# A rarely taken branch as rolled loops, and weight folds moved around it, in a two-layer attention and feed-forward kernel

## The chip, the cores and the metric

The kernel runs on one core of a Trainium2 chip. The metric is device microseconds of one execution, taken as the median of several runs. In the profile, PE is the matmul engine, PEld its weight loads, DVE the vector engine, ACT the scalar engine, POOL GpSimd, and SP the engine that issues most DMAs. A float32 matmul of the program appears as two matmul records (two passes) and two weight loads; a transpose on PE appears as one.

## The reference, cut to what matters

Eight sequences of 100 tokens, 512 wide, pass two layers. Each layer adds an attention over a context of 361 rows and then a feed-forward part.

```python
x = x + L0_xattn(layernorm(x), ctx, Wq, Wkv_expand, Wout)     # 16 heads, causal mask
x = x + L0_ffn(layernorm(x), Wg, W1, W2, W3)                  # 8 experts, best 2 of them
x = x + L1_xattn(layernorm(x), ctx, Wq, w_kc_q, w_kc_kv, W_qr, W_kr, Wo)
x = x + L1_ffn(layernorm(x), w_gate_up, w_down)               # 8-bit quantised
```

The first feed-forward part is a mixture of experts:

```python
topk_s, topk_i = top_k(x @ Wg.T, 2)
w = softmax(topk_s) spread over the 8 experts, 0 elsewhere
for e in range(8):
    y += w[..., e:e+1] * ((silu(x @ W1[e].T) * (x @ W2[e].T)) @ W3[e].T)
```

In the second attention the queries pass three matrices of a head one after the other, `Wq` (512 to 128), `w_kc_q` (128 to 384) and `W_qr` (384 to 64). Nothing stands between them, so the kernel multiplies the matrices first ("folds" them) and applies one matrix of 512 x 64 per head. The last feed-forward part uses weights that are rounded to integers row by row with a scale of their own.

## The kernel before

**Tokens and tiles.** The 800 tokens lie in seven tiles of 128 rows (the last has 32), `xs[0]` to `xs[6]`. Everything up to the experts is written in a fixed order for PE, DVE and ACT (`tc.manual_schedule`); POOL and SP are ordered by the framework's scheduler, which places a DMA where it expects its operands to be ready. Each engine then runs its own instructions strictly in the order of its program. SP's DMAs each also wait until the DMA eight before has completed.

**First attention.** Two matmuls with zeros (L433) come before the first data. Tile by tile, rows are normalised on DVE (`first_norm`), turned on PE and copied by ACT into `xnT` (`token_columns`, L253 and L254). `queries0(b, n)` (L257) makes the queries of `n` batches at once: its matmuls (L269) have `n` x 100 columns, and ACT scales and copies them (L273). Before, batches 0 and 1 are made one at a time, all others two at a time. Batch 0 needs token tile 0 alone, batch 1 tiles 0 and 1.

**Choices and slots.** `rank_choices` finds the two best experts of each token on DVE, and `give_slots` gives every choice one of 240 slots (`CAP`) of its expert; fourteen indirect DMAs of POOL (L680) write the rows into the DRAM array `x_slot`. The flag `spilt` (L806) says whether some expert has more than 240 choices. `values_load` (L879) brings it into registers of PE, DVE, ACT and POOL, and under `tc.If` (L886) a general path (L887 to L950) computes the choices without a slot: every expert over every token tile, unrolled in full, 56 times the body. With these inputs no choice is without a slot; no instruction of lines 887 to 950 but the branch itself is in the trace. Behind the branch SP reads the slot rows of experts 0 and 1 (`fetch`, L960), waiting for the last scatter.

**Folds.** Heads are folded in eight pairs, in three steps: `fold_head` for each head of a pair (L705, twelve passes of 64 columns for the pair) and a copy by ACT (L713), `fold_second` (L723, the two heads into the two column halves of the array; copy L727), and `fold_third` (four transposes, L733; copy L734) into `wqf`. `fold_load` brings a pair's matrices by SP: `wq_p` 512 KB, `kq_p` 2 x 192 KB, `qr_p` 2 x 96 KB; each has three buffers. Pair 0 is folded ahead of the branch. Of pair 1 the first step runs ahead of it (its second half is written behind it, at L1037, but the built program has all twelve passes ahead). Behind the branch come the rest of pair 1 and the whole of pair 2, then the transposes of expert 0's rows (L985), then the experts; pairs 3 to 7 are folded inside experts 0 to 4.

**Experts.** For each expert PE makes three chunks of gate and up products (`gate_and_up`, L1053), with a fold step after each, then turns the next expert's rows (L985) and multiplies by `w3` (L1117). ACT does Silu (L1064, L1072), DVE the product `hT` (L1065, L1073 to L1077). Beside it DVE quantises weights of the last feed-forward part: two rows of tiles of `w_gate_up` in each expert (`quantise_next`) and in experts 0 to 3 one tile of `w_down`, 704 KB (`quantise_down`, three long DVE instructions of 1.6, 0.95 and 0.9 us on tile `dn`, which has one buffer). DVE does that quantisation between the second and the third chunk's `hT`. SP turns each quantised tile by a DMA transpose (L150) and loads the next. SP's queue also carries the weights of the expert after the next (`load_expert`: w12 1408 KB, w3 three parts), its slot rows, the fold pairs, and `load_wo`, the output weights of the second attention, of which heads 5 to 7 use the buffers of the fold pairs.

**Later stages** (second attention, last feed-forward) follow at about 285 us.

Of the kernel before, what the change touches and what calls it, by code (L numbers as in the profile page):

```python
# [12 lines left out]
F32 = mybir.dt.float32  # L13
BF16 = mybir.dt.bfloat16
I32 = mybir.dt.int32
# [4 lines left out]
P = 128  # L20
# [30 lines left out]
def tile_kernel(  # L51
# [19 lines left out]
    def bank(dtype=F32):  # L71
        cols = 512 if dtype == F32 else 1024
        return psum.tile([P, cols], dtype, tag="bank", name="bank")
# [22 lines left out]
    SPARE = 2 * P  # L96
    x_slot = tc.dram_tile([1 + NE * CAP + 2 * NR, W], F32, name="x_slot")
    x_acc = tc.dram_tile([NR + SPARE, D], F32, name="x_acc")
    ctx_rot = tc.dram_tile([B, LP, LC, DC], F32, name="ctx_rot")
    scale_row = tc.dram_tile([OT + KC, P], F32, name="scale_row")  # L100
    xs = [keep.tile([P, D], F32, tag=f"x{t}", name=f"x{t}") for t in range(NT)]
# [155 lines left out]
    def queries0(b, n, parts=(0, 1)):  # L257
        per = 4 // n
        if parts[0] == 0:
            qT = atw.tile([P, KC, n * S], F32, tag=f"qT{n}", name=f"qT{b}")  # L260
            for i in range(n):
                queries_of[b + i] = qT[:, :, ts(i, S)]
                halves_of[b + i] = qT
        qT = halves_of[b]
        for o0 in [per * i for i in parts if per * i < KC]:
            pq = bank()
            for o in range(o0, o0 + per):
                for c in range(KC):
                    nc.tensor.matmul(  # L269
                        pq[:, ds((o - o0) * n * S, n * S)], wq_sb[:, c, ts(o, P)],  # L270
                        xnT[:, c, ds(b * S, n * S)], start=(c == 0), stop=(c == KC - 1),
                    )
            nc.scalar.activation(  # L273
                qT[:, ds(o0, per), :], pq[:, : KC * S].rearrange("p (c q) -> p c q", c=per),
                AF.Copy, scale=1.0 / math.sqrt(HD0),
            )
# [152 lines left out]
        attn0_values(b, vals.pop(b), pT)  # L429


    for _ in range(2):
        nc.tensor.matmul(bank()[:, :384], zeros[:, :P], zeros[:, :384], start=True, stop=True)  # L433
    first_norm(0, 1)
    take_columns(0)
# [1 line left out]
    first_norm(1, 2)  # L437
    keys(0, 2, KC)
    take_columns(1)
    queries0(0, 1)  # L440
    queries0(1, 1)
    first_norm(2, NT)

    begin(0)
# [257 lines left out]
    def fold_head(i, wq_p, kq_p, qr_p, j, pa=None):  # L702
        pa = bank() if pa is None else pa
        for c in range(CQ // P):
            nc.tensor.matmul(  # L705
                pa[:, ts(j, R1)], kq_p[:, j, c, :], qr_p[:, j, c, :],
                start=(c == 0), stop=(c == CQ // P - 1),
            )
        return pa

    def fold_copy(i, wq_p, kq_p, qr_p, pa):
        a_p = fw.tile([P, 2 * R1], F32, tag="a_p", name=f"a_p{i}", bufs=2)
        nc.scalar.copy(a_p, pa[:, : 2 * R1])  # L713
        return i, wq_p, a_p

    def fold_first(*loads):
        pa = fold_head(*loads, 0)
        return fold_copy(*loads, fold_head(*loads, 1, pa))

    def fold_second(i, wq_p, a_p):  # L720
        pb = bank()
        for j in range(2):
            nc.tensor.matmul(  # L723
                pb[ds(R1 * j, R1), :], a_p[:, ts(j, R1)], wq_p[:, j, :], start=True, stop=True
            )
        f_p = fw.tile([P, D], F32, tag="f_p", name=f"f_p{i}", bufs=2)
        nc.scalar.copy(f_p, pb)  # L727
        return i, f_p
# [61 lines left out]
    fold_third(*part)  # L790
    gate_scores(5, 7, xT)

    loads = loaded.pop(0)
    pa = fold_head(*loads, 0)
    rank_choices(5, 7)
    give_slots(5, 7)

# [6 lines left out]
    nc.vector.tensor_reduce(most, pn[:, :NE], AX.X, ALU.max)  # L804
    spilt = gp.tile([P, 1], I32, tag="spilt", name="spilt")
    nc.vector.tensor_scalar(spilt, most, float(CAP), None, ALU.is_gt)  # L806
    close_atw()
    close_at()

# [60 lines left out]
    def slot_tiles(e):  # L870
# [9 lines left out]
        spilt[0:1, 0:1], min_val=0, max_val=1,  # L880
        engines=[
            mybir.EngineType.PE, mybir.EngineType.DVE, mybir.EngineType.Activation,
            mybir.EngineType.Pool,
        ],
    )
    with tc.If(spills > 0, preferred_fallthrough_block=False):  # L886
        sp, close_sp = open_pool("spill", side="right")  # L887
        wts = sp.tile([P, NT, NE], F32, tag="wts", name="wts")
        for k in range(2):
            nc.vector.scalar_tensor_tensor(  # L890
                probs[k], slot1[k], 0.0, probs[k], ALU.is_equal, ALU.mult
            )
            nc.vector.tensor_tensor(
                hots[k], hots[k], probs[k].unsqueeze(2).to_broadcast([P, NT, NE]), ALU.mult
            )
        nc.vector.tensor_tensor(wts, hots[0], hots[1], ALU.add)
        for t in range(NT):
            nc.vector.memset(xs[t], 0.0)
        for e in range(NE):
            c3 = sp.tile([P, 3, D], F32, tag="sp3", name=f"sp3_{e}")  # L900
            for m, (m0, mr) in enumerate(HCH):
                nc.gpsimd.dma_start(c3[:mr, m, :], w3[e, ds(m0, mr), :])
            for t, r in enumerate(ROWS):
                pt = bank().rearrange("p (c q) -> p c q", c=KC)
                for c in range(KC):
                    nc.tensor.transpose(
                        pt[:, c, :r], x_all[:r, t, ts(c, P)], ident[:r, :r]
                    )
                xT = sp.tile([P, KC, P], F32, tag="spx", name=f"spx{e}_{t}")
                nc.scalar.copy(xT[:, :, :r], pt[:, :, :r])  # L910
                hT = sp.tile([P, 3, P], F32, tag="sph", name=f"sph{e}_{t}")
                for m, (m0, mr) in enumerate(HCH):
                    pw = bank()
                    ups = [(0, UP[m], mr)] if m < 2 else [(0, UP64, 64), (64, HE, 32)]
                    for j, cols in enumerate(([(0, m0, mr)], ups)):
                        a = sp.tile([P, KC, P], F32, tag=f"sp{j}", name=f"sp{j}_{e}_{t}_{m}")
                        for to, at_col, n in cols:
                            nc.gpsimd.dma_start(
                                a[:, :, ds(to, n)],
                                w12[e, :, ds(at_col, n)].rearrange("(c p) h -> p c h", p=P),  # L920
                            )
                        for c in range(KC):
                            nc.tensor.matmul(
                                pw[:mr, ds(j * P, r)], a[:, c, :mr], xT[:, c, :r],
                                start=(c == 0), stop=(c == KC - 1),
                            )
                    s = sp.tile([P, P], F32, tag="sps", name="sps")
                    nc.scalar.activation(s[:mr, :r], pw[:mr, :r], AF.Silu)
                    nc.vector.tensor_tensor(
                        hT[:mr, m, :r], s[:mr, :r], pw[:mr, ds(P, r)], ALU.mult  # L930
                    )
                py = bank()
                for m, (m0, mr) in enumerate(HCH):
                    nc.tensor.matmul(
                        py[:r, :D], hT[:mr, m, :r], c3[:mr, m, :], start=(m == 0), stop=(m == 2)
                    )
                nc.vector.scalar_tensor_tensor(
                    xs[t][:r], py[:r, :D], wts[:r, t, e : e + 1], xs[t][:r], ALU.mult, ALU.add
                )

        for xg in (*first_tiles[0], *first_tiles[1]):
            nc.gpsimd.memset(xg[0:1, 0:1], 0.0)
        row = sp.tile([P, NT], I32, tag="row", name="row")
        nc.gpsimd.iota(row, pattern=[[P, NT]], base=0, channel_multiplier=1)
        for t, r in enumerate(ROWS):
            nc.gpsimd.indirect_dma_start(
                out=x_acc, out_offset=bass.IndirectOffsetOnAxis(ap=row[:r, t : t + 1], axis=0),
                in_=xs[t][:r], in_offset=None, compute_op=ALU.add,
            )
        close_sp()  # L950

    close_gp()
# [81 lines left out]
    )  # L1034
    in_order.__enter__()

    part = fold_copy(*loads, fold_head(*loads, 1, pa))  # L1037
    following = fold_first(*loaded.pop(0))
    part = fold_second(*part)
    following = fold_second(*following)  # L1040
# [5 lines left out]
    for e in range(NE):  # L1046
# [35 lines left out]
        part = None  # L1082
        gate_and_up(0)
        if loaded:
            part = fold_first(*loaded.pop(0))
            if pairs_left:
                loaded.append(fold_load(pairs_left.pop(0)))
        quantise_next()
        gate_and_up(1)
        if part:  # L1090
            part = fold_second(*part)
        if e < KC:
            turn_down(*quantise_down(*down_in))
            if e + 1 < KC:
                down_in = load_down(e + 1)
        gate_and_up(2)
        quantise_next()
        if e + 2 < NE:
            experts[e + 2] = load_expert(e + 2)
        else:  # L1100
            load_wo(*((0, 1, 2) if e + 2 == NE else (3, 4)))
        if part:
            fold_third(*part)
        if e == KC + 1:
            load_wo(5, 6, 7)
        if e + 1 < NE:
            turned = columns_of(e + 1, slots[e + 1])
            gates_next = choices(e + 1, slots[e + 1])

        py = [bank() for _ in range(HC)]  # L1110
        down = [(m, i) for m in range(len(HCH)) for i in range(HC)]
# [617 lines left out]
```

## Time and profile before

| | |
|---|---|
| median of 3 runs | 683.59 us (680.39 to 683.71) |
| profiled execution | 684.2 us, of which the span is 682.5 us |
| mean granted PE clock | 0.981 |
| PE / DVE / ACT / POOL busy | 95% / 62% / 36% / 27% of the span |
| spilt flag ready on DVE (L806) | 129.16 us |
| last scatter issued (L680), first slot rows fetched (L960) | 132.96 us, 135.79 us |
| PE's first instruction behind the branch | 134.65 us |
| first product of expert 0 (L1053) | 144.27 us |
| experts 0, 1, 2 in the chain (start to next start) | 18.4, 18.2, 18.2 us |
| experts 3, 4 | 21.2, 18.4 us |
| experts 5, 6 (no fold) | 15.2 us each |

Times of instructions are counted from the span's start, and all come from the one profiled execution. A row of the timeline gives start, duration, engine, line, operation, tiles and count, and in brackets the idle time before it with what ended it. A row of the question by source line gives least, median and greatest duration in ns. A row of the windows gives, for a stretch, the busy time and number of instructions of PE, PEld, DVE, ACT and POOL, then the granted PE clock, the DMA share (1.0 when all 16 DMA engines are busy) and GB/s. DMA work that an instruction starts is not inside that instruction's duration. PE's busy time counts modelled ends, so neighbouring rows overlap a little; the chain of waits counts each stretch once.

### The profile page before, as it was taken

How to read it: one execution, taken by the hardware profiler on the slowest of the kernel's cores; microseconds unless marked ns; L12 is line 12 of the kernel's file. 1: busy time of each engine (PE TensorE's matmuls, PEld its weight loads, DVE VectorE, ACT ScalarE, POOL GpSimd, SP SyncE). 2: the span in 40 equal slices, each digit the busy share in tenths (PEclk: the TensorE clock that was granted, in tenths of full speed). 3: DMA queues.
4: the chain of work that ended last, by engine and by line, in shares of the span. 5: the costliest groups of instructions: out<-in, count | busy, mean ns of one | idle time of the engine just before them, and what ended most of it. 6: DMA issues, size and time to landing. Idle time of an engine off the chain costs nothing.

```text
span 682.5 us, 10210 instructions
## 1 busy us (share of the span) xinstructions
PE 647.0 (95%) x3637; PEld 417.3 (61%) x3637; DVE 420.7 (62%) x1059; ACT 245.2 (36%) x557; POOL 184.1 (27%) x197
## 2 busy tenths in 40 slices
PE   8999997499998999999999999999999999999995
PEld 6767755367765677568866666666666644444442
DVE  4875698326665453254168877776676356566687
ACT  3654444141221211231155555455555322221140
POOL 2222231601110022138424243324333102221021
PEclk9999999589999999999999999999999999999998
DMA  8700293699999999664200211110000120111211
GB/s 303 237 17 18 99 331 108 244 301 190 271 288 321 322 254 275 131 193 122 63 1 17 57 44 42 31 35 12 1 11 1 46 83 8 30 29 30 49 37 61
DMA packets 80312, 80.41 MB, mean 118 GB/s; under 512 B 41283, under 2 KB 54135, under 8 KB 80127
## 3 DMA queue, kind: packets, MB, share of 16 engines
q1 hardware_dynamic: 76543, 70.97, 35.8%
q0 software_dynamic: 3712, 8.72, 6.6%
q8 instruction: 30, 0.49, 0.3%
q14 instruction: 27, 0.22, 0.1%
HBM read 56.36 MB, written 16.50 MB: 107 GB/s over the span
## 4 chain that ended last, share of the span: by engine, by line
PE 65%; DVE 7%; DMA 3%; POOL 2%; issue 2%; ACT 1%; SPq 0%; POOLq 0%; ACTq 0%; DVEq 0%
PE bank L357 12%; PE bank L1053 10%; PE bank L1333 10%; PE bank L1312 7%; PE bank L1267 6%; PE bank L1117 5%; PE bank L1327 4%; PE bank L1457 3%; POOL e L1321 2%; PE bank L1300 2%; DVE nm L1314 1%; PE bank L705 1%; PE bank L723 1%; DMA dn<-in_wdn 1%; PE bank L985 1%
## 5 line engine op out<-in xcount | busy, mean ns | idle before, releaser
L1321 POOL TENSOR_SCALAR e<-e,rs 128x361 f32<-128x361 f32 (+1 forms) x56 | 67.3, 1203 | 134.9 <-DVE rs L1320 134.2
L357 PE MATMUL bank<-wvo,ctxT 128*128 128x512 f32 x192 | 83.9, 593 | 0.0
L1312 PE MATMUL bank<-kvT,qe 128*128 128x361 f32 (+1 forms) x208 | 82.0, 477 | 0.0
L1053 PE MATMUL bank<-xgT,w 128*128 128x240 f32 (+1 forms) x384 | 76.5, 371 | 1.6 <-ACT xgT L989 0.9
L1053 PEld LDWEIGHTS bank<-xgT,w 128*128 128x128 f32 (+1 forms) x384 | 63.8, 181 | 16.7 <-issue 9.0
L1333 PE MATMUL bank<-pT,kvr 121*128 121x400 f32 x192 | 70.4, 502 | 1.8 <-DVE pT L80 1.8
L1318 ACT ACTIVATE e<-bank,nm 128x361 f32<-128x361 f32 (+1 forms) x104 | 58.7, 564 | 29.8 <-DVE nm L1314 21.0
L1327 PEld LDWEIGHTS bank<-ident,e 128*121 128x121 f32 (+1 forms) x312 | 47.3, 183 | 33.7 <-POOL e L1321 7.8
L1314 DVE TENSOR_REDUCE nm<-bank 128x1 f32<-128x361 f32 (+1 forms) x104 | 54.9, 528 | 20.3 <-PE bank L1312 19.2
L357 PEld LDWEIGHTS bank<-wvo,ctxT 128*128 128x128 f32 x192 | 36.2, 190 | 43.1 <-issue 42.6
L1128 POOL DMA_INDIRECT x_acc<-y,place x16 | 24.4, 1525 | 128.5 <-ACT y L1127 125.0
L1327 PE MATMUL bank<-ident,e 128*121 128x128 f32 (+1 forms) x312 | 52.8, 279 | 2.1 <-POOL e L1321 2.1
L1474 POOL TENSOR_TENSOR hid<-g,u 128x512 f32<-128x512 f32 (+1 forms) x17 | 20.5, 1214 | 111.1 <-ACT g L1465 74.8
L1333 PEld LDWEIGHTS bank<-pT,kvr 121*128 121x128 f32 x192 | 33.9, 190 | 21.3 <-issue 1.9
L1117 PE MATMUL bank<-w,hT 128*128 128x512 f32 (+3 forms) x96 | 43.3, 596 | 2.2 <-DVE hT L1077 2.2
L1267 PE MATMUL bank<-xT,wqf 128*128 128x256 f32 (+1 forms) x192 | 43.8, 389 | 0.7 <-ACT xT L1252 0.7
L322 POOL TENSOR_TENSOR s<-s,rs 100x800 f32<-100x800 f32 x16 | 24.4, 1523 | 71.2 <-DVE rs L321 30.5
L1267 PEld LDWEIGHTS bank<-xT,wqf 128*128 128x128 f32 x192 | 36.2, 190 | 7.4 <-ACT xT L1252 0.9
L1312 PEld LDWEIGHTS bank<-kvT,qe 128*128 128x128 f32 (+1 forms) x208 | 32.5, 186 | 9.4
L82 ACT COPY pT<-bank 121x384 f32<-121x384 f32 (+1 forms) x51 | 23.7, 465 | 31.9 <-PE bank L1327 31.3
L80 DVE COPY ctxT<-bank 128x400 f32<-128x400 f32 (+2 forms) x23 | 13.2, 574 | 34.1 <-PE bank L1267 24.8
L1117 PEld LDWEIGHTS bank<-w,hT 128*128 128x128 f32 (+3 forms) x96 | 16.8, 183 | 22.9 <-issue 16.4
(251 smaller groups left out, 1020.2 us busy)
## 6 DMA issues: line engine op xcount, KB each, us to landing
w<-in_w SPq DMA_DIRECT2D x8, 1408.0 KB
gu<-in_wgu SPq DMA_DIRECT2D x22, 256.0 KB
w<-in_w SPq DMA_DIRECT2D x16, 256.0 KB
wq_p<-in_wq SPq DMA_DIRECT2D x8, 512.0 KB
wo<-in_wo SPq DMA_DIRECT2D x8, 512.0 KB
x_slot<-zeros SPq DMA_DIRECT2D x1, 3840.0 KB
kq_p<-in_wkcq SPq DMA_DIRECT2D x16, 192.0 KB
dn<-in_wdn SPq DMA_DIRECT2D x4, 704.0 KB
```

The costliest lines, as they stand in the source:

```text
L322: nc.gpsimd.tensor_tensor(part, part, rs.unsqueeze(2).to_broadcast([S, 8, S]), ALU.mult)
L357: nc.tensor.matmul(po[:, :D], lhs[:, c, ds(t * P, r)], rhs[:, c, :], start=(c == 0), stop=(c == chunks - 1),)
L1053: nc.tensor.matmul(po, w12_e[:, c, cols], xgT[:, c, :], start=(c == c0), stop=(c == c1 - 1))
L1117: nc.tensor.matmul(py[i][:n], hT[:mr, m, ds(s0, n)], w3_e[:mr, m, :], start=(m == 0), stop=(m == 2))
L1128: d = nc.gpsimd.indirect_dma_start(out=x_acc, out_offset=bass.IndirectOffsetOnAxis(ap=place[:, 0:1], axis=0), in_=y, in_offset=None, compu ...
L1267: nc.tensor.matmul(pq[:, i, :], wqf[:, c, ts(p0 + i, P)], xT[:, c, :], start=(c == 0), stop=(c == KC - 1),)
L1312: nc.tensor.matmul(ps[:r, :L], qe[:, ds(k0, r)], kvT, start=True, stop=True)
L1314: d = nc.vector.tensor_reduce(nm[:r], ps[:r, :L], AX.X, ALU.max, negate=True)
L1318: nc.scalar.activation(e[:r], ps[:r, :L], AF.Exp, bias=nm[:r], accum_out=sm[:r])
L1321: (nc.vector if odd else nc.gpsimd).tensor_scalar_mul(e[:r], e[:r], rs[:r])
L1327: nc.tensor.transpose(pt[:LP, c, :r], e[:r, ds(c * (LP - 1), LP)], ident[:r, :r])
L1333: nc.tensor.matmul(pc[:, :VC], kvr[:, c, :], pT[:, c, ts(j, VC)], start=(c == 0), stop=(c == LC - 1))
```

## The change

1. One more matmul with zeros at the start (three for two).
2. Queries of batches 0 and 1 are made together, as those of the later batches.
3. Pair 1 is folded whole ahead of the branch: first step before `rank_choices(5, 7)`, second and third after the flag is computed. Behind the branch stand pairs 2 and 3; pairs 4 to 7 are folded in experts 0 to 3, and expert 4 has none.
4. Inside the experts the first step has new functions. `fold_beside` swaps the operands: `qr_p` (64 columns) is now the weight and `kq_p` (128 columns) streams, and the two heads of a pair go into the two column halves of the array. The result lies turned, so `fold_turn` turns it back: one transpose and one more copy by ACT per pair. Each later step of a pair moves one place down: the second step after the third chunk, the third after the next expert's transposes.
5. The general path is written as two rolled loops over experts and token tiles, with gathers by indirect DMA, and adds into `x_acc` directly. SP takes part in the branch, so it too loads the flag. The body is now the path that falls through.
6. ACT runs a Silu on one column behind the branch, which the built program places ahead of it together with its table load.

```diff
-    for _ in range(2):
+    for _ in range(3):
         nc.tensor.matmul(bank()[:, :384], zeros[:, :P], zeros[:, :384], start=True, stop=True)
...
-    queries0(0, 1)
-    queries0(1, 1)
+    queries0(0, 2)
...
+    def fold_beside(i, wq_p, kq_p, qr_p):
+        pa = bank()
+        for c in range(CQ // P):
+            for j in range(2):
+                nc.tensor.matmul(
+                    pa[ds(R1 * j, R1), :P], qr_p[:, j, c, :], kq_p[:, j, c, :],
+                    start=(c == 0), stop=(c == CQ // P - 1),
+                )
+        t_p = fw.tile([P, P], F32, tag="t_p", name=f"t_p{i}", bufs=1)
+        nc.scalar.copy(t_p, pa[:, :P])
+        return i, wq_p, t_p
+
+    def fold_turn(i, wq_p, t_p):
+        pa = bank()
+        nc.tensor.transpose(pa[:, :P], t_p, ident)
+        a_p = fw.tile([P, P], F32, tag="a_p", name=f"a_p{i}", bufs=2)
+        nc.scalar.copy(a_p, pa[:, :P])
+        return i, wq_p, a_p
...
-    loads = loaded.pop(0)
-    pa = fold_head(*loads, 0)
+    part = fold_first(*loaded.pop(0))
     rank_choices(5, 7)
     give_slots(5, 7)
...
+    part = fold_second(*part)
+    fold_third(*part)
     close_atw()
...
-            mybir.EngineType.Pool,
+            mybir.EngineType.Pool, mybir.EngineType.SP,
...
-    with tc.If(spills > 0, preferred_fallthrough_block=False):
+    with tc.If(spills > 0, preferred_fallthrough_block=True):
...
-            for t, r in enumerate(ROWS):
+        with tc.For_i(0, NE, 1, hint_engines=()):
...
+            with tc.For_i(0, NT, 1, hint_engines=()):
+                x_t = sp.tile([P, D], F32, tag="spx", name="spx")
+                gathered(x_t, x_all_rows, at_x)
...
-    part = fold_copy(*loads, fold_head(*loads, 1, pa))
+    nc.scalar.activation(most, ln_eps, AF.Silu)
+    part = fold_first(*loaded.pop(0))
     following = fold_first(*loaded.pop(0))
...
         gate_and_up(0)
         if loaded:
-            part = fold_first(*loaded.pop(0))
+            part = fold_beside(*loaded.pop(0))
...
         gate_and_up(1)
         if part:
-            part = fold_second(*part)
+            part = fold_turn(*part)
...
         gate_and_up(2)
+        if part:
+            part = fold_second(*part)
         quantise_next()
...
-        if part:
-            fold_third(*part)
...
             turned = columns_of(e + 1, slots[e + 1])
             gates_next = choices(e + 1, slots[e + 1])
+        if part:
+            fold_third(*part)
```

The order of SP's DMAs is not written by hand. In the built program it shifts inside the experts: before, SP's queue in expert 2 reads turned `dn` tile 2, load of `dn` tile 3, turned and loaded `w_gate_up` tiles, w12 of expert 4; after, it reads load of a `wo` part, w12 of expert 4, turned `dn` tile 2, load of `dn` tile 3. Likewise in expert 1: before, turned `dn` tile 1, load of `dn` tile 2, and then w12 of expert 3; after, `wq_p` of pair 7, w12 of expert 3, turned `dn` tile 1, load of `dn` tile 2. In expert 0, w12 of expert 2 stands ahead of `dn` tile 1 in both; after, `wq_p` of pair 6 stands ahead of it too.

## The prediction

> **What bounds the kernel now.** I read the page's busy shares first (PE 95% of 682.5 us), then the 40 slices, where the granted clock falls to 5 and 8 tenths in slices 8 and 9 (119 to 153 us) and the DMA share is full from slice 10 to 15. So two stretches matter: the branch, and the experts behind it. The rows on the branch, from the questions by source line and by time:
>
> ```profile
> L886 ACTq COMPARE_BRANCH  x2: 38/44/49, 130.0 to 130.1; - x2
> L886 PEldq COMPARE_BRANCH  x2: 89/1917/3745, 130.4 to 130.7; - x2
> ...
> 134.65 2.64 PEld L705 LDWEIGHTS bank<-qr_p,kq_p 128*128 128x128 f32 x12 [8.12 <-issue]
> 137.40 3.74 PE L723 MATMUL bank<-wq_p,a_p 128*64 128x512 f32 x8
> 142.37 0.98 PE L985 MATMUL bank<-ident,xg 128*128 128x128 f32 x8
> ```
>
> PE's second branch instruction, a jump over the body of the general path, holds PE for 3.745 us; ScalarE's takes 49 ns. PE restarts at 134.65, cold (granted clock 0.50 from 121 to 141), and the folds then run without a gap into the first expert's transposes.
>
> Behind it the chain of waits, cut to its pieces, shows the one place where an expert does not wait for PE:
>
> ```profile
> 199.09 3.45 PE bank L1053 x16
> ...
> 204.44 7.48 DMA dn<-in_wdn
> ...
> 211.94 1.63 DVE amax L145
> ```
>
> ```profile
> 156.00:158.00 2.00, 2.00 (x16) 1.70 (x15) 1.89 (x5) 1.44 (x3) 0.00 (x0) 1.00 0.35 52
> 188.00:196.00 8.00, 8.00 (x42) 4.81 (x41) 5.47 (x10) 2.40 (x5) 0.00 (x0) 1.00 1.11 313
> 196.00:204.00 8.00, 8.00 (x38) 5.77 (x37) 5.13 (x16) 1.21 (x3) 3.04 (x2) 1.00 1.15 270
> ```
>
> The last row of `w_down` lands at 211.92. VectorE, in written order, cannot multiply expert 3's third hidden chunk before it has quantised that row, and PE stands 1.89 us at L1117. Expert 3 took 21.2 us (199.1 to 220.3), experts 1 and 2 took 18.2. The last two columns of the windows are DMA share and GB/s: in 188 to 204 the queue is full, in 156 to 158 it has a hole. So from 135.8 on one DMA queue, SP's, runs beside PE, and expert 3 ends when the queue has got through its list.
>
> **The change part by part.** *Start.* The third warm-up product costs two passes of 0.73 us (L433, 4 in 2.93) and lies in PE's 1.32 us gap before L253: 0.14 us too long. The queries of batches 0 and 1 go from 64 passes in 7.29 us (L269, 10.25 to 17.54) to 32 passes, which for batches 2 and 3 took 5.68. But they now need tile 1's columns, and ScalarE's copy of them ends at 11.03; before, batch 0 ran ahead of it. 11.1 + 5.68 = 16.78, so 0.76 is won, 0.62 after the warm-up. The second copy and the scale of tiles 2 to 6 (17.98 on ScalarE, released by PE) move with it, and nothing up to the scatters waits for a DMA. Bounds: 0 to -1.6. I take **-0.65** for all that follows, the scatters and SP's row fetch at 135.79 among it.
>
> *Branch.* The rolled body is some 200 PE instructions instead of thousands. The Trainium skill, "Runtime: NRT & Kernel Launch", section "Instruction fetch mechanics", says that fetch is sequential, and that a taken branch to a target outside a window of two blocks of 256 instructions waits for a DMA fetch, hence the advice to unroll. Read as advice it speaks against loops; read with the row, the unrolled body pays the 3.7 us. By the row alone, a jump that fits costs what ScalarE's does, 0.05. Nothing in the trace shows a short jump on PE, so the bounds are 0 and -3.7; I take -3.7. SP, which had no branch to test, now loads the flag as well: the other engines took 1.2 us from 129.2 (TENSOR_LOAD 0.5 to 0.8 plus the test), and SP stands until 135.79 for the last scatter anyway. That cover is over 4 us.
>
> *Folds behind the branch.* Pair 1's second and third step move ahead of it, into PE's idle 126.6 to 130.7; pair 3 comes in whole. So 12 L705 passes are added, 2.80 us cold. PE would restart at 130.9: 5.6 for two firsts, then seconds and thirds. How long it stays cold matters. "TensorE: Matmul & The Clock Gate", section on the HAM clock gate, gives about 3.4 us of activity until the clock is back; here it took some 6.4 (134.65 to 141.x). By the page the folds would take 2.80 + 0.6 + 1.0 + 2.0 + 0.8 = 7.2 us, by the row 5.6 + 0.8 + 1.6 + 1.1 = 9.1. The trace decides: 130.9 + 9.1 = 140.0 against 142.54, **-2.55**. The rows of the slots, fetched from 135.8, have landed by 142.3 at the latest and, at the scatters' 3.2 us from issue to landing, by 139.5 (an estimate), so PE is still last. The early Silu table load takes 1.28 us from ScalarE at 143.73 and the one at 137.55; both lay under PE's passes, so nothing.
>
> *Experts 0 to 3.* A first step costs 1.28 us warm. With column halves two 64-column passes share the array: six pairs of 128 columns at 0.85 ns (L357: 437 ns for 512) are 0.66, and L723, halves already, takes 1.01 for 4 passes where 0.87 is ideal; L1053's half passes lose 0.36. I take 0.9 (0.66 to 1.28) and 0.11 for the new transpose: **-0.27 each, -1.1**. The two small ScalarE copies (0.27 each) lie beside 3 us of passes. *Expert 4* has no fold left: 18.43 against expert 5's 15.21, **-3.2**.
>
> On PE alone: -0.65 - 2.55 - 1.1 - 3.2 = **-7.5 us**.
>
> *SP's queue.* Here it is lost again. Compared in program order, the queue of the changed kernel asks for pair 6's `wq` ahead of expert 2's weights, and at each later expert puts the weights w12 and a `wq_p` load **ahead of** the turned row and the next `dn`. Before, the last `dn` had P4 to P7 and the weights of experts 2 and 3 in front of it; now also w12 of expert 4 (1408 KB) and `wo` for head pair 5 (512 KB): 1.97 MB, at 360 GB/s (212 to 220: 368) +5.5 us. Against that, the hole at 156 to 158.5, where SP waited for PE to free a weight buffer, fills: 2.2 to 2.7, I take 2.5. With the start, the last `dn` lands at 211.9 - 0.65 + 5.5 - 2.5 = 214.3. From its landing to the end of expert 4 were 26.8 us (211.94 to 238.74); less the fold, 23.6: 237.9, **-0.85**. PE alone would be there at 231.2. The later wins.
>
> The third `dn` shifts likewise: from 190.65 to about 193, while PE, earlier, wants it by about 187: a stand of some 6 us in expert 2, then 3 in expert 3. Experts 5 to 7 have weights early. The later stages hold the same instructions.
>
> **Sum.** 684.2 us of the profiled run - 0.9 = 683.3; the runs' median lies 0.6 lower, so **682.6**. Up to 3.4 us (0.5%) a measurement of this kernel does not tell from none; the three runs themselves spread over 3.3.
>
> **Rivals.**
> - *PE's gains reach the end* (676.0): expert 3 stands as long as now, because the added bytes go into holes or transposes that hold the ring hardly slow down others. -7.5, median 676. For it: the queue ran at 25 to 65 GB/s in 163 to 165 and 168 to 171, so bytes are not all that it is short of. Against: 184 to 243 hardly has a hole. 0.33.
> - *The longer stands cool PE* (687.5), the other side: if PE idles[...] at L1117 in expert 3, its clock halves, as it did at 121 after PE had worked 1.0 of 3.3 us, and 1.7 to 3.4 us are lost; with nothing filled in the hole (+2.5) that gives -0.85 + 2.5 + 2.5 = +4.2.[...] For it: the stand worked out for expert 3 is about that long. Against: a cold spell in expert 2 is eaten by expert 3's wait. 0.24.
> - *The jump stays slow* (683): the branch costs as before. The queue decides all the same, so nothing changes; it is within the forecast. 0.08.
> - *The forecast*, -4 to +2.5: 0.35.
>
> **Numbers.** Range 8 in 10: **674.5 to 688.0**; the likeliest alone 679.5 to 685.5. Faster: the first rival and the forecast's lower edge, 0.38; within: 0.35; slower: the second and the upper edge, 0.27.
>
> **What would show it.** PE's jump under 0.5 us and L705 from about 130 on; first expert at about 141; the `dn` wait of expert 2 at 5 to 6 us and of expert 3 at 3, the last `dn` landing at about 214; expert 4 at 15.2 us; L726 below 1.0 us for 12 passes. If the `dn` waits are not longer than before, the queue's order costs nothing and the first rival holds. If PE's jump still takes over 3 us, the step on the branch is wrong; if granted clock falls below 1.00 in 195 to 225, the second rival is at work.

## The result, and the profile after

| | before | after |
|---|---|---|
| median | 682.14 us (680.39 to 683.71, 8 runs) | 678.19 us (676.95 to 679.45, 8 runs) |
| span of the profiled execution | 682.5 us | 677.3 us |
| first product of expert 0 | 144.27 us | 142.20 us |
| experts 0, 1, 2, 3, 4 in the chain | 18.4, 18.2, 18.2, 21.2, 18.4 us | 22.9, 17.6, 17.6, 17.6, 15.2 us |

The changed kernel takes 0.9937 of the time before, with a 95% interval of 0.9923 to 0.9951: about 4.3 us less. A gain of 0.9 us was forecast. The time of 682.6 was too high, and it stood on the wrong reason.

The line numbers move: L705 is now L706, L723 is L744, L985 is L1035, L1053 is L1104, L1117 is L1170; L726 is the first fold step inside the experts (`fold_beside`), L736 its turn back. The branch of the changed kernel, from the questions by source line and by time:

```profile
L908 PEldq COMPARE_BRANCH  x1: 353/353/353, 129.4 to 129.4; - x1
```

```profile
130.19 5.36 PE L706 MATMUL bank<-qr_p,kq_p 128*128 128x64 f32 x24 [0.30 <-PEq L908]
135.48 3.58 PE L744 MATMUL bank<-wq_p,a_p 128*64 128x512 f32 x8
...
140.30 0.98 PE L1035 MATMUL bank<-ident,xg 128*128 128x128 f32 x8
142.20 3.48 PE L1104 MATMUL bank<-xgT,w 128*128 128x240 f32 x16 [0.92 <-ACT xgT L1039]
147.45 0.40 PE L726 MATMUL bank<-kq_p,qr_p 128*64 128x128 f32 x2 [1.78 <-DMA qr_p<-in_wqr]
149.09 1.54 PE L726 MATMUL bank<-kq_p,qr_p 128*64 128x128 f32 x10 [1.23 <-DMA qr_p<-in_wqr]
150.56 4.44 PE L1104 MATMUL bank<-xgT,w 128*128 128x240 f32 x16
```

PE's jump of 3.745 us is 0.353 now, and PE restarts 4.5 us earlier. But the folds behind the branch take 10.1 us (130.19 to 140.30) where one and a half pairs took 7.7. In expert 0 the brackets show what nothing before had shown: PE stands twice, 1.78 and 1.23 us, for `qr_p` of pair 4. And the products behind that stand take 4.44 us where the same 16 passes take 3.5 elsewhere. The windows tell why (PEclk, DMA share and GB/s are the last three columns):

```profile
146.00:148.00 2.00, 0.40 (x2) 0.19 (x2) 1.78 (x5) 0.08 (x1) 0.00 (x0) 1.00 1.14 282
148.00:150.00 2.00, 0.91 (x9) 0.91 (x10) 0.45 (x2) 0.00 (x0) 0.00 (x0) 0.77 1.06 265
150.00:152.00 2.00, 2.00 (x8) 1.48 (x7) 0.00 (x0) 0.27 (x1) 0.00 (x0) 0.50 1.22 288
```

PE works 0.4 of 2 us, and the granted clock then falls to 0.50 for the products that follow. Now the chain of waits, in expert 0 and from expert 3 on:

```profile
141.74 7.31 DMA qr_p<-in_wqr
...
200.34 3.24 PE bank L1104 x16
203.58 0.81 PE bank L726 x12
204.39 3.44 PE bank L1104 x16
...
217.95 9.07 PE bank L1104 x48
```

The chain runs through the load of `qr_p`, which SP issues at 141.74, behind the slot rows; and `dn<-in_wdn`, which held expert 3 before, is not in it at all. Start to start, the sum is: first expert -2.07, expert 0 +4.49, experts 1 and 2 -0.59 and -0.58, expert 3 -3.61, expert 4 -3.22, together -5.58. Two questions follow: was the new wait in expert 0 the whole loss, and why was the `dn` wait gone when the prediction had it grow?

### The profile page after: what moved, and what is told of

Its sections match the earlier page's. It is cut to its first block, busy times and chain, and to the rows that moved or that the text cites. A ratio compares the mean times of both kernels' runs of the same rounds, so it can differ in the third digit from the quotient of the medians.

```text
span 677.3 us, 10150 instructions
## 1 busy us (share of the span) xinstructions
PE 648.4 (96%) x3604; PEld 418.0 (62%) x3611; DVE 419.4 (62%) x1059; ACT 245.4 (36%) x561; POOL 184.2 (27%) x197
## 4 chain that ended last, share of the span: by engine, by line
PE 65%; DVE 6%; DMA 4%; POOL 2%; issue 1%; SPq 1%; ACT 1%; POOLq 0%; ACTq 0%; DVEq 0%
PE bank L359 12%; PE bank L1104 10%; PE bank L1386 10%; PE bank L1365 8%; PE bank L1320 6%; PE bank L1170 6%; PE bank L1380 4%; PE bank L1510 3%; POOL e L1374 2%; PE bank L1353 2%; DVE nm L1367 1%; DMA qr_p<-in_wqr 1%; PE bank L1035 1%; DMA gu<-in_wgu 1%; DMA x_acc<-y,place 1%
## 5 line engine op out<-in xcount | busy, mean ns | idle before, releaser
L1104 PE MATMUL bank<-xgT,w 128*128 128x240 f32 (+1 forms) x384 | 76.4, 372 | 0.9 <-ACT xgT L1039 0.9
L1104 PEld LDWEIGHTS bank<-xgT,w 128*128 128x128 f32 (+1 forms) x384 | 64.8, 183 | 12.7 <-issue 6.7
L1170 PE MATMUL bank<-w,hT 128*128 128x512 f32 (+3 forms) x96 | 43.0, 595 | 0.3 <-DVE hT L1128 0.3
L1116 DVE TENSOR_TENSOR hT<-silu,bank 128x240 f32<-128x240 f32 x16 | 6.5, 405 | 41.9 <-ACT silu L1115 41.9
```

The lines of the kernel that those rows point to most:

```text
L1104: nc.tensor.matmul(po, w12_e[:, c, cols], xgT[:, c, :], start=(c == c0), stop=(c == c1 - 1))
L1170: nc.tensor.matmul(py[i][:n], hT[:mr, m, ds(s0, n)], w3_e[:mr, m, :], start=(m == 0), stop=(m == 2))
```

## The experiments

The groups of runs stood on chips whose times for the kernel before differ (medians 682.8, 685.8 and 685.1 us), so kernels are compared through their ratios to the kernel before in the same group.

### The wait in expert 0

**Pair 4 early.** One line is added, ahead of the branch:

```diff
     part = fold_second(*part)
+    loaded.append(fold_load(pairs_left.pop(0)))
     fold_third(*part)
```

> The changed kernel, but the matrices of pair 4 are asked for ahead of the branch (behind the second step of pair 1, which frees their buffer) and no longer behind it. Theory (late load): expert 0 takes 22.9 us in the changed kernel because L726 waits for `qr_p` of pair 4, whose load SP can only issue at about 138, behind the slot rows. With the load early that wait is gone, the granted clock stays at 1.00 in 145 to 155, expert 0 takes 17.6 us like experts 1 to 3, and all of the 5.3 us reaches the end: about 672.8 us, ratio to before 0.985 to 0.987. Rival (queue, as the prediction had it): PE then wants the last `dn` 5 us earlier, a `dn` wait of 2 to 5 us comes up in expert 3, and the ratio stays at 0.991 to 0.994.

0.9909 (0.9878 to 0.9941). In its profile expert 0 takes 17.7 us, without a wait at L726, and the span is 673.3 us, 4.0 below the changed kernel's. But the interval overlaps the changed kernel's (two of its seven runs lie at 678.5 and 681.5), and a `dn` wait of 1.5 us was there in expert 3. So both kernels were run again, side by side.

> The changed kernel once more, beside the three runs that follow, which differ from it or from each other by one thing. Late-load theory: again PE waits for `qr_p` of pair 4 in expert 0 (22 to 23 us against 17.6 for experts 1 to 3), whatever the chip; ratio 0.992 to 0.995. If that wait was chance, expert 0 takes less than 20 us here and the ratio falls below 0.990.

> The changed kernel with pair 4 loaded ahead of the branch, once more, since its first ratio (0.988 to 0.994) did not part from the changed kernel's. Late-load theory: 3 to 5 us below the changed kernel of the same call, ratio to before 0.986 to 0.990. Rival (the gain is lost to the `dn` wait): within 1.5 us of the changed kernel.

The changed kernel: 0.9949 (0.9931 to 0.9967), median 682.39. Pair 4 early: 0.9886 (0.9869 to 0.9904), median 677.82, 4.6 us less. The intervals part. Expert 0 in this execution of the changed kernel, and in the kernel with pair 4 early, by time:

```profile
150.25 0.40 PE L726 MATMUL bank<-kq_p,qr_p 128*64 128x128 f32 x2 [1.50 <-DMA qr_p<-in_wqr]
151.72 0.87 PE L726 MATMUL bank<-kq_p,qr_p 128*64 128x128 f32 x10 [1.06 <-DMA qr_p<-in_wqr]
152.52 3.51 PE L1104 MATMUL bank<-xgT,w 128*128 128x240 f32 x16
```

```profile
148.95 0.88 PE L726 MATMUL bank<-kq_p,qr_p 128*64 128x128 f32 x12
```

The wait belongs to the changed kernel; its size does not. Here PE stood 2.6 us, the clock stayed at 1.00, the products behind took 3.51 us, and expert 0 took 20.7 us, where I had expected 22 to 23. In the first profile it stood 3.0 us, the clock fell, and expert 0 took 22.9. So the late load costs some 3.1 us, and 5.3 where the clock falls with it. The execution profiled here was a quick one (680.2 us, with a median of 682.4), which fits the 4.6 us between the medians. With pair 4 early, expert 0 takes 17.7. This version beats both kernels.

**Pair 3 in expert 0.** Pair 3 is not folded behind the branch but in expert 0, where its matrices have long been there:

```diff
-    following = fold_first(*loaded.pop(0))
...
-    following = fold_second(*following)
...
-    fold_third(*following)
```

> The changed kernel, but pair 3 is folded in expert 0 again (pairs 3 to 7 in experts 0 to 4) and only pair 2 stands behind the branch; as a consequence the scheduler leaves SP's order as it was before (turned row and `dn` ahead of w12). Late-load theory: pair 3 is long loaded when expert 0 wants it, so expert 0 takes 17.6 to 18 us and not 22.9; the first expert starts at 140 to 142 all the same, since the slot rows land at about 139; expert 4 has a fold again (17.6, not 15.2). Sum against the changed kernel: -5 + 2.4 - 0.5 = about -3 us, ratio to before 0.988 to 0.991. Rival: PE is idle and cold ahead of expert 0 and loses there what it gains, ratio 0.993 to 0.996.

0.9969 (0.9950 to 0.9988): the rival. L726 runs without a wait (0.88 us for 12 passes), so the first half of the theory holds. But with one fold fewer PE has gaps from 126 to 142 us and starts expert 0 cold:

```profile
130.16 1.97 PE L744 MATMUL bank<-wq_p,a_p 128*64 128x512 f32 x4 [3.79 <-ACT a_p L714]
...
143.92 4.93 PE L1101 MATMUL bank<-xgT,w 128*128 128x240 f32 x16 [0.92 <-ACT xgT L1039]
...
217.17 2.46 PE L1167 MATMUL bank<-w,hT 96*128 96x512 f32 x4 [2.27 <-DVE hT L1125]
219.83 4.52 PE L1101 MATMUL bank<-xgT,w 128*128 128x240 f32 x16 [0.21 <-issue]
```

16 passes in 4.93 us instead of 3.48; the first expert starts at 143.92 and takes 19.1 us. The gap of 3.79 us is not the missing fold's doing: the profile with pair 4 early, of the last group, has one of 3.36 us at the same place. But there the folds of two pairs then run from 133.75 with no gap over 0.2 us, and by the trace's clock records the full clock is back at 142.0; here it is back at 146.9. The second fold behind the branch thus also warms PE up. Besides, VectorE waited 5.3 us in two experts for `dn`. In expert 3 PE stood 2.27 us for it, the granted clock read 0.50 from 218.5 to 222.0, and experts 3 and 4 took 21.1 and 18.7 us. This run has SP's old order, too, so its `dn` waits are no measure of the fold alone.

### The `dn` wait and SP's queue

**Before, once more.** Is the wait that bounded expert 3 in the first profile part of the kernel?

> The kernel before, unchanged, profiled once more. In the first profile PE waits 1.9 us in expert 3 for the last `dn`, and the DMA engines move only 25 to 98 GB/s in 162 to 165 and 33 to 91 GB/s in 168 to 172. If these stretches belong to the kernel's order, they are here again at the same places, and expert 3 takes 21.2 us again. If they are chance (single packets that take 2 to 3 us), they lie elsewhere or are shorter, and expert 3 takes anything between 18.2 and 21 us.

It is not there. First the chain of this execution in experts 3 and 4, then its tile `dn`:

```profile
205.63 3.24 PE bank L1053 x16
...
223.83 3.24 PE bank L1053 x16
```

```profile
L145 DVE TENSOR_REDUCE amax<-dn x4: 1612/1612/1614, 159.6 to 214.3; 128x1 f32<-128x1408 f32 x4
...
its engine sat idle before it (us, times) until:
who waited for it (us, times):
```

In the first profile the same view had a wait:

```profile
L145 DVE TENSOR_REDUCE amax<-dn x4: 1614/1620/1621, 153.1 to 211.9; 128x1 f32<-128x1408 f32 x4
...
its engine sat idle before it (us, times) until:
  DMA dn<-in_wdn: 5.0, 2
```

All stands some 6.5 us later in the second execution (the first expert starts at 150.82), but expert 3 takes 18.2 us like its neighbours, and the list of waits for `dn` is empty. PE had not simply fallen behind the queue: SP's first row fetch is 5.9 us later too (141.65 against 135.79), and yet SP issues the last `dn` only 0.8 us later (205.25 against 204.44). The profiles with the branch alone and with the start alone, whose queue has the same order, wait 0.4 and 0.6 us. What differs lies in the DMA engines. The windows of the first profile of before, one us each:

```profile
162.00:163.00 1.00, 1.00 (x5) 0.62 (x4) 0.38 (x3) 0.57 (x1) 0.16 (x1) 1.00 3.57 98
163.00:164.00 1.00, 1.00 (x7) 0.94 (x6) 0.49 (x1) 0.00 (x0) 1.00 (x1) 1.00 0.06 25
164.00:165.00 1.00, 1.00 (x7) 0.94 (x6) 0.00 (x0) 0.00 (x0) 0.70 (x2) 1.00 0.13 34
...
168.00:169.00 1.00, 1.00 (x7) 0.94 (x6) 0.72 (x2) 0.00 (x0) 0.00 (x0) 1.00 2.47 65
```

A share of 3.57 in one us means that packets which began in it held the engines for 3.57 us: by the DMA records, 19 packets of 256 bytes took 2.2 to 2.9 us here, where most take 0.02. In the two stretches, 162 to 165 and 168 to 172, seven windows lie under 100 GB/s. In the second execution the hole of 156 to 158 lies at 162 to 165; from there to 212 one window alone is under 130 (204 to 205, with 83), and no packet takes over 2 us. The profiles with the branch alone and with the start alone have low windows as well, at most two in a row behind the hole. So some 5 to 6 us of the queue's time in the first profile belong to that execution and not to the order; what made the packets slow stays open. The 18 runs of the kernel before in the first group spread from 680.3 to 685.3 us.

**The queue's order.** Two runs change the order of SP's queue in the kernel before. In the first, the turned row and the next `dn` load are only held behind w12:

```diff
+            with tc.issue_after(w12_load[0]):
+                turn_down(*down_q)
+                if e + 1 < KC:
+                    down_in = load_down(e + 1)
```

> The kernel before with one part of the change alone: in experts 0 to 3 the turned row of `w_down` and the load of the next `dn` stand behind the w12 of the expert after the next in SP's queue, as they do in the changed kernel; nothing else differs. Bytes theory (the prediction's step): 1.4 MB more ahead of the last `dn` makes it land about 4 us later, at 215 to 216, PE's wait in expert 3 grows from 1.9 to about 5 us, the kernel is 2 to 4 us slower, ratio 1.003 to 1.006. Transposes theory: the DMA transposes leave the ring nearly idle when nothing stands beside them (29 to 50 GB/s in 163 to 171), and with a large load in flight they cost next to nothing; the last `dn` lands no later than 211, the wait in expert 3 is gone, expert 3 takes 18.2 us, ratio 0.995 to 0.997.

1.0127 (1.0099 to 1.0155), slower than either theory said. The scheduler had put the load behind more than w12: behind the second `w_gate_up` row's turn and w3 too. Its chain of waits in expert 2:

```profile
183.53 0.62 DVE xgT L989
186.84 4.05 SPq L150
190.93 6.08 DMA dn<-in_wdn
197.03 1.63 DVE amax L145
```

VectorE frees the turn (L150) only when it has got through expert 1 and turned rows for expert 2; SP then loads `dn` behind the turn, and VectorE needs that `dn` to get through expert 2. This is a ring of waits, not a sum of bytes: experts 0 to 3 take 18.3, 19.9, 21.1 and 22.1 us, and VectorE waits 10.3 us in all. So this run answers a harsher question than asked. The second has the order of the changed kernel: in experts 1 and 2 w12, turned row, `dn`, the `w_gate_up` row, w3:

```diff
+        w12_load[0] = nc.sync.dma_start(a, w12[e].rearrange("(c p) h -> p c h", p=P)).ins
+        if between:
+            with tc.issue_after(w12_load[0]):
+                behind = between()
+            with tc.issue_after(behind):
+                quantise_next()
...
+        def down_moves():
+            turn_down(*down_q)
+            if e + 1 < KC:
+                next_down.append(load_down(e + 1))
+            return dn_load[0]
```

> The kernel before with SP's order of the changed kernel: in experts 1 and 2 the weights w12 stand right ahead of the turned row and the next `dn`, then the second `w_gate_up` row, then w3 (the run before this one had the `dn` load behind w3 and the `w_gate_up` row as well, and was 1.3% slower). Bytes theory, as the prediction had it: 1.4 MB more ahead of the last `dn`, some 3.9 us at 360 GB/s, expert 3 waits 4 to 6 us, the kernel is 2 to 4 us slower, ratio 1.003 to 1.006. Slack theory: once w12 is in flight the turn and the load follow in time, the `dn` wait is no longer than before, ratio 0.996 to 1.001.

1.001 (0.998 to 1.004), and no wait for `dn`. The slack theory holds: SP issues the last `dn` load 0.4 us before expert 3 starts (203.41 and 203.84), in the second execution of before 0.2 us (205.25 and 205.47). The 1.4 MB that the prediction charged at the rate of the queue cost nothing that the interval shows.

Two more runs move `dn` at the faster pace of the kernel with pair 4 early. In one, w12 stands behind `dn` as before:

```diff
+        if e + 1 < KC:
+            with tc.issue_after(dn_load[0]):
+                experts[e + 2] = load_expert(e + 2)
```

> The run with pair 4 early, but w12 of the expert after the next stands behind the next `dn` load in SP's queue, as in the kernel before (the scheduler then also moves the last fold pair and one output weight ahead of `dn`). It tests the queue's order at the pace of 17.6 us an expert. Bytes theory, as the prediction had it: `dn` lands 2 to 4 us earlier, no `dn` wait is left, ratio 0.5 to 1 us better than the run with pair 4 early. Order theory: w12 waits behind the transposes and then pushes slot rows, fold pairs and the next `dn` back by an expert's time; the `dn` wait in expert 3 grows to 2 us or more, as in the run with pair 3 in expert 0, and the kernel is 1 to 3 us slower.

0.9891 (0.9873 to 0.9909) against 0.9886: neither theory; there is no `dn` wait in either profile. In the other, the `dn` load goes ahead of the transpose:

```diff
-            turn_down(*quantise_down(*down_in))
+            down_q = quantise_down(*down_in)
             if e + 1 < KC:
                 down_in = load_down(e + 1)
+                with tc.issue_after(dn_load[0]):
+                    turn_down(*down_q)
```

> The changed kernel with pair 4 loaded ahead of the branch (as in the run of that name), and the next `dn` load ahead of the DMA transpose of the row before it, behind w12. There PE was early enough for `dn` to wait again, 1.5 us in expert 3, because SP's issue of the transpose takes 3.8 to 4.7 us while w12 is in flight and the load stands behind it. Theory: the load issues 4 us earlier, the wait of expert 3 is gone, the experts take 17.6 us each, and the kernel gains 0.5 to 1.5 us on that run: ratio to before 0.987 to 0.990. Rival: the load only shares the DMA engines with w12, lands when it did, and nothing changes (0.990 to 0.992).

0.9884 (0.9862 to 0.9906), within what the theory gave but no better than pair 4 early alone in the run beside the changed kernel. The load did issue earlier, but one transpose then held SP 9.28 us, and VectorE waited 1.4 us for it instead. Small moves of `dn` are worth nothing that I could measure.

### Parts of the change alone

**The branch alone.** The kernel before with the rolled loops only:

```diff
-            mybir.EngineType.Pool,
+            mybir.EngineType.Pool, mybir.EngineType.SP,
...
-    with tc.If(spills > 0, preferred_fallthrough_block=False):
+    with tc.If(spills > 0, preferred_fallthrough_block=True):
...
+        with tc.For_i(0, NE, 1, hint_engines=()):
```

> The kernel before with one part of the change alone: the general path as rolled loops, SP in the branch, the body falling through. Folds, start and queue order stay as before. Jump theory: PE's last branch instruction takes 0.35 us in place of 3.745, PE restarts at about 130.9, experts 0 to 2 start 3.5 us earlier. Then two views part. PE view: the gain reaches the end, -3.5 us, ratio 0.994 to 0.996. Queue view: the last `dn` lands where it did, at 211.9 (less the hole at 156 to 158 that fills), so PE's wait in expert 3 grows from 1.9 to 4 us or more, and the end moves by -0.5 to -2 us, ratio 0.997 to 0.999.

0.9942 (0.9921 to 0.9963): the PE view. The branch instruction takes 0.353 us, and the last `dn` is waited for 0.4 us, not 4, although PE is earlier. SP's first row fetch was 0.8 us later than in the first profile of before (136.61 against 135.79) and yet the last `dn` was quantised 6.0 us earlier (205.9 against 211.9): the same queue in the same order, without the two stalls. This run takes as much off as the whole change does (0.9937 and 0.9949), and the start alone takes off 2.1 us: without the late load of pair 4 the change would be worth more, and with pair 4 early it is (0.9886). Rolling the loops and letting the body fall through came together in every run, so what each is worth is not shown.

**The start alone.**

```diff
-    for _ in range(2):
+    for _ in range(3):
...
-    queries0(0, 1)
-    queries0(1, 1)
+    queries0(0, 2)
```

> The kernel before with the start alone: a third product with zeros, and the queries of batches 0 and 1 made together. The prediction priced this at -0.65 us (0 to -1.6); the changed kernel's trace has the scores 1.17 us and the first scatter 1.15 us earlier, which would be -1.2. If all comes from these two edits, the first scatter stands at about 115.0 here too (116.18 before). At the end: -1.2 us if nothing takes it back, ratio 0.998; if the last `dn` binds expert 3, it is SP's start that counts, and expert 3's wait is about the same as before. Rival: the shift comes from elsewhere in the changed kernel (order of DMAs at the start), and the first scatter stays within 0.3 us of 116.18, ratio 1.000.

0.9969 (0.9956 to 0.9982), so about 2.1 us, more than expected. The reason shows only when executions are laid side by side. The second executions of before and of the changed kernel, by time:

```profile
1.51 2.93 PE L433 MATMUL bank<-zeros 128*128 128x384 f32 x4 [1.51 <-POOL zeros L161]
6.11 1.09 PE L253 MATMUL bank<-ident,xn 128*128 128x128 f32 x4 [1.68 <-DVE xn L244]
6.99 4.84 PE L224 MATMUL bank<-ctx,wkv_sb 128*128 128x400 f32 x8
```

```profile
1.51 4.21 PE L435 MATMUL bank<-zeros 128*128 128x384 f32 x6 [1.51 <-POOL zeros L163]
5.70 0.98 PE L255 MATMUL bank<-ident,xn 128*128 128x128 f32 x4
6.51 2.85 PE L226 MATMUL bank<-ctx,wkv_sb 128*128 128x400 f32 x8
```

With two products of zeros PE stands 1.68 us, and the eight passes of the context's keys take 4.84 us; with three it does not stand, and they take 2.85. In the five profiles with the old start they took 2.92 to 4.84 us (the first profile of before was the quickest), in the nine with the new one 2.85 to 3.29: 1.1 us less on the mean. The first scores (L296, L298) started at 18.15, 19.32, 19.52, 19.66 and 19.99 us in the five profiles with the old start, and at 16.91 to 17.81 (mean 17.3) in the nine with the new one: 2.0 us on the mean. The clock makes the difference in the keys. Single passes take 0.874 us at first and 0.499 us later, and the first record of the full clock in the trace stands at 5.0, 9.1, 9.4, 9.7 and 11.0 us with the old start, and at 4.4 to 7.5 us with the new one; the later it stands, the more passes are slow (none at 5.0, over five at 11.0). The windows, which count time ahead of the first record as 1.00, hide this. That the third product brings the full clock sooner because PE works longer without a pause is argued: no run has that product without the joined queries.

**The column halves undone.** Pair 4 early, with the old first step inside the experts:

```diff
-            part = fold_beside(*loaded.pop(0))
+            part = fold_first(*loaded.pop(0))
...
-        if part:
-            part = fold_turn(*part)
```

> The run with pair 4 early, but the first fold step inside experts 0 to 3 as it was before (twelve 64-column passes, no column halves, no turn back); the places of the later steps stay. It prices the column halves. By the prediction they are worth 0.27 us an expert, 1.1 us in four; by the trace, where experts 1 to 3 take 17.61 us against 18.20, 0.59 us an expert, 2.4 us, of which the first step alone is 1.28 - 0.81 - 0.11 = 0.36. Expected: experts 0 to 3 at 17.9 to 18.1 us, the whole 1.4 to 2 us slower than the run with pair 4 early. Rival: with PE slower the `dn` wait of expert 3 is gone, so only 0.5 to 1 us is lost.

0.9906 (0.9887 to 0.9924) against 0.9886; the intervals overlap, but the chains of the two are even: experts 1 to 3 take 17.83 us here and 17.61 with the halves. They are worth 0.22 us an expert. The other 0.37 of the 0.59 us by which experts 1 and 2 became shorter is still there without them, so it comes from the later places of the second and third step, which I had counted at nothing. The chain shows it: before, the last two chunks of products took 3.30 and 2.79 us with the second step (1.01) between them; in this run they take 5.88 together, and the second step behind them 0.86.

## Why the prediction was off, step by step

The forecast of 682.6 lies 4.4 us above the median measured (its sum, 683.3 less 0.6, gives 682.7). Its own range (679.5 to 685.5) misses it by 1.3 us; the wide range holds it, on the side of the rival "PE's gains reach the end" (676.0), whose mechanism is nearer to what happened.

- **Branch.** Right in size: 3.745 us became 0.353, and PE restarted at 130.19 (130.9 predicted). The run of this part alone gives 0.9942, some 4 us. That instruction fetch is the cause, no run shows.
- **Folds behind it.** Mis-sized: 9.1 us predicted, 10.1 measured. By the trace's clock records the full clock came back 8.6 us after the restart (it averages 0.79 over 138 to 140), and 9.9 in the second execution; before it was 6.9, and 6.4 in the run with the branch alone (restart at 132.34, 0.81 over the same 2 us). Why it takes longer here is not shown. The trace had rightly been taken over "TensorE: Matmul & The Clock Gate", section on the HAM clock gate, whose 3.4 us are off still further. Branch and folds together gave -0.92 (-2.07 less the start's -1.15), not -2.55.
- **Experts 0 to 3.** The halves: 0.27 predicted, 0.22 measured. The moved steps gave 0.37 more, a term that the prediction put at nothing. **Expert 4**: -3.22 (-3.2 predicted).
- **Expert 0.** The step that was missed. "The rows of the slots ... have landed by 142.3" and "PE is still last" followed PE to the first expert and stopped there. The change folds one pair more behind the branch, so the pair that expert 0 needs is no longer one that was loaded long before, but pair 4, which SP can ask for only at 138 to 142. Nothing in the prediction asks when `qr_p` of pair 4 lands. Price: 3.1 to 5.3 us by two profiles; 4.6 us between the medians of the runs with and without it.
- **SP's queue.** The step that failed. "1.97 MB, at 360 GB/s +5.5 us ... the last `dn` lands at 214.3" was to undo PE's 7.5 us. In the changed kernel VectorE began on it at 208.64 without a wait (210.3 in the second execution, after a wait of 0.6). The order alone costs nothing (1.001, 0.998 to 1.004). The base of the step was wrong too: the landing at 211.9 came from two DMA stalls of one execution, and another has no `dn` wait. The rival named the stretches of 25 to 65 GB/s; they should have decided.
- **Start.** Mis-sized: 0.65 predicted, 2.0 to 2.1 by fourteen profiles and the run alone. Faster passes of the keys (1.1 us), where the full clock comes sooner, were put at nothing. The profile from which it was priced was the quickest of five.
- **Clock.** "The longer stands cool PE" was right as a mechanism and had the wrong place: in the changed kernel stands of 3.0 us in all took the clock down, in expert 0 and for another tile. In two runs it struck in expert 3, as described: the clock read 0.50 for 3.4 us behind stands of 1.76 us (`dn` held behind w12) and 2.27 us (pair 3 in expert 0). Stands of 1.89 us before and of 2.6 us in the second execution left it at 1.00, so the length of a stand alone did not decide. Ahead of the fall at 121, PE was busy for 1.5 of 3.3 us in the windows, not 1.0.

Two errors thus met: a loss that was charged and was not there (the queue) stood in for one that was there and not seen (pair 4). That the wide range still held is owed in part to this luck.

## What to carry to other kernels

When a piece of prefetched work is moved forward by one place, ask of every consumer behind it which load it now needs, and when that load is issued; a queue's order that stays as it was can be one item too late. Before a wait of one or two us is taken for the bound, look at it in a second execution, or at the transfer rate around it: a bound returns, a stall does not. And bytes ahead of a load cost time only where the load has no slack; count from when it is wanted.

## What the runs showed of the hardware that I had not expected

- The jump over the unrolled body took PE 3.745, 3.925, 3.970, 4.045 and 4.185 us in five profiles of kernels with it; over the rolled body, which also falls through, it took 0.352 or 0.353 us in all nine.
- Single DMA packets of 256 and 2048 bytes took 2.1 to 2.9 us at 162 and 168 us in one execution (27 of them), with the engines at 25 to 98 GB/s meanwhile, and the same kernel had none over 2 us from 140 to 215 in the next. The runs of the branch alone and the start alone had two and five.
- The granted clock fell to 0.50 in an expert behind stands of PE of 1.76, 2.27 and 3.0 us, and not behind stands of 1.89 and 2.6 us.
- In all eight profiles of the two later groups, whatever the kernel, ScalarE stood 6.4 to 7.8 us, instead of the 3.65 of the six earlier ones, in front of the copy of the second pair (L713 before) and the exponential behind it (L630); from the first scatter of the slots to the last it then took 19.4 to 20.6 us, not 16.8. The kernel before is 2.3 to 2.9 us slower in these groups than in the first. The profile names only a remote releaser; this stays open.
